# Latent attention with an output layer: VectorE and ScalarE in program order in three of four query blocks, with other tile sets and a later rotary stack

## The chip, the cores and the metric

The kernel runs on one core of a Trainium2 chip. A core has TensorE (PE: matrix products; its weight loads are listed as PEld), VectorE (DVE), ScalarE (ACT), GpSimd (POOL) and SyncE (SP, which here issues most DMAs). Each engine runs its own queue of instructions; semaphores tie them together. The metric is the device time of one execution in microseconds (us). Most executions agree within 0.3%.

## The reference

One transformer layer on x of 2048 rows and 512 columns, all in float32. Cut to what matters:

```python
cq = rms_norm(x @ w_qa.T, q_a_ln_w)                  # latent query, 384
q_nope, q_pe = split((cq @ w_qb.T), 16 heads)        # 128 and 64 per head
ckv = x @ w_kva.T                                    # latent 128 and rotary key 64
k_nope, v = split(rms_norm(ckv[:, :128]) @ w_kvb.T)  # 128 and 128 per head
scores = (q_nope @ k_nope.T + rot(q_pe) @ rot(k_pe).T) * scale, causal
out = softmax(scores) @ v
x = layernorm(x + concat(out) @ w_o.T)
x = layernorm(x + x @ (weight * scale_weight).T + bias)
```

## The kernel before

**What is computed where.** The up-projection of the keys is folded into the query weights, and the one of the values into the output weights (tile `wvo`, made by `value_output` from `wo` and `wv`). So all heads share one latent key and one latent value, and a head's score is a product of its projected query (`qn`) with the latent keys `Kn` plus a product of its rotary query (`pe`) with `Kp`. A float32 factor is split into a high and a low part, and three products replace one. The softmax probabilities become a high and a low float16 half.

**How the work is cut.** The queries fall into four blocks b of 512 rows, the 16 heads into eight pairs p, a block into four query tiles qt of 128 rows. `units` (L609) runs over p, then qt, then the two heads j. One head's 128 queries are called a unit here: a pair has eight units, numbered 2 qt + j. A unit of block b looks at nk = 128 (4b + qt + 1) keys: 128 to 512 in block 0, up to 1024 in block 1, 1536 in block 2, 2048 in block 3.

**A unit, stage by stage.** `head_scores` (L420): PE writes the scores into one or two PSUM tiles of up to 1024 keys (L409, five products for each 512 keys); DVE adds the causal mask where PE has not (L415), takes the row's maximum of each tile (L442) and makes the bias from it (L449 or L451); ACT takes the exponential `pr` of each tile and its sum (L457); DVE makes `inv` from the sums (L467 or L469) and its reciprocal (L470). `head_probs` (L473): ACT writes the high half of `hl` (L478), DVE the low half (L481), both in two cuts when nk is above 1024, and a DMA on SP's queue transposes `hl` into a ring in SBUF (L485). `head_scores` is given the generator of the unit before (`prev`) and draws its steps in among its own. `values` (L534), one to three query tiles later, multiplies the transposed probabilities with V on PE, ACT copies the result `ot` (L539), and a DMA stores it.

**Fillers.** While a pair is worked on, the next pair's queries are projected a piece at a time: `fill` is called after the units whose number is in the list `at`. `project_nope` (L368) has two pieces, one head each (PE L379, then a split by ACT L66 and DVE L67). `project_pe` (L323) has two pieces and serves two pairs at once; after its products on DVE (L340), POOL builds the rotary stack `pe` (L347 to L362) with one copy by ACT (`ph`, L350). At a block's last pair the next block's latent query `cq` and the weights `wq` and `wpe` are loaded on the way (`load_block`, `load_wq`, `load_wpe`). In block 3's last pair the fillers are two pieces of `value_output` (L177), and `prepare_output` (L724) loads `wo` and the first stored results and splits them.

**What sets the order.** Block 0 is ordered by the program's scheduler on all engines. Blocks 1 to 3, and the value projections that start the tail, stand in a `manual_schedule` for PE and SP: these two issue in program order, while the scheduler orders DVE, ACT and POOL by its own estimate. In the tail, PE again runs in a written order: `accumulate` (L743) sums the heads' results times `wvo`, then the normalisation and the second linear layer follow.

**Buffers.** Blocks 1 and 3 have three score tiles of two PSUM banks, block 2 has two of these and two of one bank, and two banks are left for projections and values. All SBUF tiles of a unit in blocks 1 to 3 (`pr`, `hl`) come from the pool `blk13` with two buffers each, beside the ring.

Of the kernel before, what the change touches and what calls it, by code (L numbers as in the profile page):

```python
# [19 lines left out]
P = 128  # L20
# [29 lines left out]
def mla_block(ctx: ExitStack, tc: tile.TileContext, a, out):  # L50
# [272 lines left out]
    def project_pe(b, g, direct=None):  # L323

        if direct is None and ("wpe", b, g) not in state:
            load_wpe(b, g)
        w = state.pop(("wpe", b, g)) if direct is None else direct
        cq, cs = state["cq"], state["cs"]
        prod = prj.tile([P, 2, 2, QB], F32, tag="prod", name=f"prod{b}_{g}")
        for x in range(2):  # L330
            ps = psum["m"].tile([P, QB], F32, tag="m", name=f"ps_pe{b}_{g}_{x}")
            n = 0
            for lt in range(LT):
                for i, k in ((0, 0), (0, 1), (1, 0)):
                    nc.tensor.matmul(  # L335
                        ps, w[:, i, lt, x * P : (x + 1) * P], cq[:, k, lt, :], start=n == 0, stop=n == 8
                    )
                    n += 1
            for k in range(2):
                nc.vector.tensor_tensor(prod[:, k, x, :], ps, cs[:, k ^ x, :], ALU.mult)  # L340
            if x == 0:
                yield
            elif b or g == 3:
                load_wpe(*((b, g + 1) if g < 3 else (b + 1, 0)))
        rp, tp = prod[:, 0], prod[:, 1]
        eng = nc.vector if (b, g) == (0, 0) else nc.gpsimd
        eng.tensor_tensor(rp[:, 0, :], rp[:, 0, :], rp[:, 1, :], ALU.subtract)  # L347
        eng.tensor_tensor(rp[:, 1, :], tp[:, 0, :], tp[:, 1, :], ALU.add)
        ph = prj.tile([P, 2, QB], F32R, tag="ph", name=f"ph{b}_{g}")
        nc.scalar.activation(ph, rp, AF.Copy)  # L350
        pe = blk.tile([P, 4, QB], F32R, tag="pe", name=f"pe{b}_{g}")

        quick = b == 0 or (b, g) == (1, 0)
        for j in range(4):
            q = slice(32 * j, 32 * j + 32)
            for x in range(2):
                to = pe[32 * x : 32 * x + 32, j, :]
                if quick:
                    nc.scalar.activation(to, rp[q, x, :], AF.Copy)
                else:  # L360
                    nc.gpsimd.tensor_copy(to, rp[q, x, :])
                (nc.gpsimd if not quick or (b, g) == (0, 0) and j % 2 else nc.vector).tensor_tensor(  # L362
                    pe[64 + 32 * x : 96 + 32 * x, j, :], rp[q, x, :], ph[q, x, :].bitcast(F32), ALU.subtract
                )
        state["pe", b, g] = pe
        yield

    def project_nope(b, p, direct=None):  # L368
# [5 lines left out]
        for j in range(2):  # L374
            ps = psum["m"].tile([P, QB], F32, tag="m", name=f"ps_qn{b}_{p}_{j}")
            n = 0
            for lt in range(LT):
                for i, k in ((0, 0), (0, 1), (1, 0)):
                    nc.tensor.matmul(  # L379
                        ps, w[:, i, lt, j * P : (j + 1) * P], cq[:, k, lt, :], start=n == 0, stop=n == 8  # L380
                    )
                    n += 1
            split(ps, qn[:, 0, j, :], qn[:, 1, j, :], kvln)
            if j == 1:
                state["qn", b, p] = qn
                if b or p == NPAIR - 1:
                    load_wq(*((b, p + 1) if p + 1 < NPAIR else (b + 1, 0)))
                if p == NPAIR - 1:
                    load_block(b + 1)
            yield  # L390

    def project(b, p):
# [27 lines left out]
    def head_scores(pool, b, p, j, qt, nk, prev):  # L420
# [6 lines left out]
        for ti, ck in enumerate(cks):  # L427

            if b == 2 and ti == 1:
                ps = psum["t"].tile([P, 1, 512], F32, tag="t", name=f"s{b}_{p}_{qt}_{j}_{ti}", bufs=2)  # L430
            else:
                ps = psum["s"].tile(
                    [P, 2, 512], F32, tag="s", name=f"s{b}_{p}_{qt}_{j}_{ti}", bufs=2 if b == 2 else 3
                )
            w = ck[0][1]
            for ci, (c0, w) in enumerate(ck):
# [14 lines left out]
            nc.vector.tensor_scalar(bias, neg[:, 0:1], neg[:, 1:2], r, ALU.min, ALU.mult)  # L451
        for _ in prev:
            pass
        pr = pool.tile([P, nk], F32, tag="pr", name=f"pr{b}_{p}_{qt}_{j}")
        sums = small.tile([P, 2], F32, tag="sums", name="sums")
        for ti, (v, c0, n, w) in enumerate(tiles):
            nc.scalar.activation(  # L457
# [151 lines left out]
    def units(pool, ring, b):  # L609
        lag = min(ring.shape[1] // (2048 * (b + 1)) - 1, 3)  # L610

        for p in range(NPAIR):
# [24 lines left out]
            for qt in range(4):  # L637
# [78 lines left out]

    cuts = {}

    def load_wo(g, tag):
        w = blk.tile([P, 4, HID], F32, tag=tag, name=f"wo{g}")  # L720
        nc.sync.dma_start(w, a["wo"][:, 4 * g : 4 * g + 4])  # L721
        state.setdefault("wo", []).extend(w[:, j] for j in range(4))

    def prepare_output(b, p, k):  # L724
# [39 lines left out]
    blk13 = ctx_m.enter_context(tc.tile_pool(name="blk13", bufs=2, reuse_waits="tile"))  # L764
    ring = blk13.tile([P, 12 * 2048], F16, name="ring", bufs=1)
    side[:] = []
    state["queue"] = nc.sync
    with tc.manual_schedule(engines={mybir.EngineType.PE, mybir.EngineType.SP}):
        for b in range(1, NB):
            with ExitStack() as ctx_s:  # L770
                for k in ("t", "s") if b == 2 else "s":
                    psum[k] = ctx_s.enter_context(
                        tc.tile_pool(name=f"ps_{k}{b}", bufs=1, space=PSUM, reuse_waits="tile")
                    )
                units(blk13, ring, b)

        flush()
        ps_a = ctx.enter_context(tc.tile_pool(name="ps_a", bufs=4, space=PSUM, reuse_waits="tile"))
# [20 lines left out]
    wvo += [pc.tile([P, 2, 2, HID], F32R, name=f"wvo{p}") for p in range(EARLY, NPAIR)]  # L799
    fsc = pc.tile([P, HID], F32, name="fsc")  # L800
    nc.gpsimd.dma_start(fsc, a["fsc"].partition_broadcast(P))
    fb = pc.tile([P, HID], F32, name="fb")
# [53 lines left out]
            if late and next(late[0], None) is None:  # L856
                late.pop(0)

    ET = mybir.EngineType
# [97 lines left out]
```

## Time and profile before

Times of three runs: 1638.54, 1638.7 and 1641.59 us, median 1638.7. The profiled execution is another one:

| what | us |
|---|---|
| profiled execution, its own time | 1642.03 |
| its span in the profile | 1640.2 |
| PE busy | 1562.4 (95%) |
| PEld busy | 1294.7 (79%) |
| DVE busy | 1161.8 (71%) |
| ACT busy | 929.0 (57%) |
| POOL busy | 360.5 (22%) |

The span runs from the first to the last recorded instruction; the execution's time holds 1.8 us more around it. Shares are of the span. Below, a time such as 876.83 is a place in the span. A line such as `PE s L409 <- ACT pr L457: 16.9, 16, 3.6` says that PE, before its instructions of L409 that write `s`, waited for ACT's L457 for 16.9 us in all, in 16 waits, the longest 3.6 us. A timeline line has start, length, engine, line, operation and tiles, and in brackets the idle time before it and what ended that. In the rows by stage, the clock is the one granted to TensorE, 1.00 for full speed.

### The profile page before, as it was taken

Reading aid. Unit: us, or ns where it says so; the run is one execution under the profiler, and the core shown is the slowest. Engines: PE = TensorE matmul, PEld = TensorE weight load, DVE = VectorE, ACT = ScalarE, POOL = GpSimd, SP = SyncE. Lnnn points to the kernel's source line nnn. Section 1 sums busy time; section 2 is a strip of 40 time slices with the busy share of each in tenths; the row PEclk is TensorE's granted clock in tenths of the full one; section 3 lists DMA queues with packets and bytes.
Section 4 is the critical chain, followed back from the end, with each engine's and each line's share of the span. In section 5 each row is a group of like instructions: output and inputs, shape, how many; then the busy total and the mean of one; then the engine's idle time right before and its main releaser. Section 6 shows DMA issues by size and latency. Waiting matters only on the chain. (4 is left out here: it accounts for less than half of the span.)

```text
span 1640.2 us, 24716 instructions
## 1 busy us (share of the span) xinstructions
PE 1562.4 (95%) x9130; PEld 1294.7 (79%) x9130; DVE 1161.8 (71%) x2099; ACT 929.0 (57%) x1631; POOL 360.5 (22%) x434
## 2 busy tenths in 40 slices
PE   8898999999998999999999999999999999999997
PEld 7787877788877888888887787787887777688876
DVE  5677777887778888887787777777777674455554
ACT  5667666666655676766665565565566564311120
POOL 2232324153105405050033202201300000022132
PEclk9899999999999999999999999999999999999999
DMA  6789677788887878888898687786788698433230
GB/s 213 218 218 235 169 186 166 144 168 170 162 189 158 177 160 167 159 165 167 175 187 165 128 162 151 143 157 138 143 155 168 133 183 209 145 114 122 91 109 32
DMA packets 633031, 262.48 MB, mean 160 GB/s; under 512 B 570288, under 2 KB 611376, under 8 KB 631888
## 3 DMA queue, kind: packets, MB, share of 16 engines
q1 hardware_dynamic: 621472, 233.62, 66.4%
q0 software_dynamic: 4672, 17.73, 3.5%
q10 hardware_dynamic: 6768, 9.57, 2.0%
q8 instruction: 72, 1.18, 0.3%
q14 instruction: 47, 0.39, 0.1%
HBM read 83.17 MB, written 35.13 MB: 72 GB/s over the span
## 5 line engine op out<-in xcount | busy, mean ns | idle before, releaser
L409 PE MATMUL s<-Kn,qn 128*128 128x512 f32 (+4 forms) x1920 | 522.9, 378 | 29.6 <-ACT pr L457 27.3
L457 ACT ACTIVATE pr<-s,bias,rq 128x1024 f32<-128x1024 f32 (+3 forms) x320 | 324.3, 1017 | 142.4 <-DVE bias L451 101.5
L409 PEld LDWEIGHTS s<-Kn,qn 128*128 128x128 f32 x1920 | 338.8, 190 | 83.3 <-ACT pr L457 39.6
L534 PE MATMUL o<-ring,V 128*128 128x256 f16 x3252 | 393.6, 273 | 6.9 <-ACT ot L539 3.7
L481 DVE SCALAR_TENSOR_TENSOR hl<-pr,inv,hl 128x1024 f16<-128x1024 f32 (+7 forms) x320 | 357.4, 1137 | 60.3 <-ACT hl L478 58.9
L478 ACT ACTIVATE hl<-pr,inv 128x1024 f16<-128x1024 f32 (+7 forms) x320 | 295.4, 961 | 167.9 <-DMA ring<-hl 60.9
L534 PEld LDWEIGHTS <-V 128*128 128x128 f16 x3264 | 302.7, 98 | 86.6 <-issue 47.3
L442 DVE TENSOR_REDUCE neg<-s 128x1 f32<-128x1024 f32 (+3 forms) x320 | 318.5, 996 | 71.0 <-PE s L409 66.5
L409 PE MATMUL s<-Kp,pe 128*128 128x512 f32 (+4 forms) x1280 | 361.4, 363 | 0.0
L409 PEld LDWEIGHTS s<-Kp,pe 128*128 128x128 f32 x1280 | 234.0, 189 | 29.6
L347 POOL TENSOR_TENSOR prod<-prod 128x512 f32<-128x512 f32 x15 | 19.3, 1284 | 662.2 <-DVE prod L340 662.2
L379 PE MATMUL ps_qn<-cq,wq 128*128 128x512 f32 x576 | 147.0, 401 | 5.1 <-ACT ot L539 4.3
L743 PE MATMUL acc<-wvo,oh 128*128 128x512 f32 x448 | 145.4, 406 | 0.0
L362 POOL TENSOR_TENSOR pe<-prod,ph 32x512 fp32r<-32x512 f32 x92 | 140.7, 1530 | 11.0 <-issue 5.1
L379 PEld LDWEIGHTS ps_qn<-cq,wq 128*128 128x128 f32 x576 | 108.4, 192 | 26.7 <-ACT ot L539 4.8
L743 PEld LDWEIGHTS acc<-wvo,oh 128*128 128x128 f32 x448 | 84.7, 191 | 21.4 <-issue 2.9
L743 PE MATMUL acc<-wvo,ol 128*128 128x512 f32 x224 | 89.2, 398 | 0.0
L469 DVE TENSOR_SCALAR inv<-sums 128x1 f32<-128x1 f32 x128 | 26.9, 210 | 80.1 <-ACT pr L457 80.0
L64 DVE TENSOR_TENSOR ol<-o,oh 128x1024 fp32r<-128x1024 f32 x28 | 38.5, 1376 | 62.6 <-ACT oh L63 62.6
L63 ACT ACTIVATE oh<-o 128x1024 fp32r<-128x1024 f32 x28 | 29.7, 1060 | 93.4 <-PE acc L743 54.1
L335 PE MATMUL ps_pe<-cq,wpe 128*128 128x512 f32 x288 | 71.9, 394 | 3.8 <-DMA cq<-cq_d 3.8
L539 ACT ACTIVATE ot<-o 128x256 f32<-128x256 f32 x128 | 48.1, 377 | 46.0 <-PE o L534 45.9
(140 smaller groups left out, 1608.3 us busy)
## 6 DMA issues: line engine op xcount, KB each, us to landing
wq<-wq_d SPq DMA_DIRECT2D x22, 768.0 KB, 5.6
o<-ot_d SPq DMA_DIRECT2D x32, 512.0 KB, 3.3
ot_d<-ot SPq DMA_DIRECT2D x97, 128.0 KB, 2.5
wpe<-wpe_d SPq DMA_DIRECT2D x10, 768.0 KB, 5.1
wq<-wq_d POOLq DMA_DIRECT2D x9, 768.0 KB, 6.0
wq_d<-wst SPq DMA_DIRECT2D x9, 512.0 KB, 5.0
cq_d<-cqst SPq DMA_DIRECT2D x18, 256.0 KB, 3.8
wo<-in_wo_dram SPq DMA_DIRECT2D x4, 1024.0 KB, 8.2
```

The source lines that it names most:

```text
L64: nc.vector.tensor_tensor(l, ps, h.bitcast(F32), ALU.subtract)
L335: nc.tensor.matmul(ps, w[:, i, lt, x * P : (x + 1) * P], cq[:, k, lt, :], start=n == 0, stop=n == 8)
L362: (nc.gpsimd if not quick or (b, g) == (0, 0) and j % 2 else nc.vector).tensor_tensor(pe[64 + 32 * x : 96 + 32 * x, j, :], rp[q, x, :], ph ...
L379: nc.tensor.matmul(ps, w[:, i, lt, j * P : (j + 1) * P], cq[:, k, lt, :], start=n == 0, stop=n == 8)
L409: nc.tensor.matmul(ps[:, :w], lhs, K[:, i, c0 : c0 + w], start=n == 0, stop=n == 4)
L442: nc.vector.tensor_reduce(neg[:, ti : ti + 1], v, axis=AX.XY, op=ALU.max, negate=True)
L457: nc.scalar.activation(pr[:, c0 : c0 + n * w].rearrange("p (a c) -> p a c", a=n), v, AF.Exp, bias=bias, scale=r, accum_out=sums[:, ti : ti ...
L478: nc.scalar.activation(hl[:, 0, c], pr[:, c], AF.Copy, scale=inv)
L481: nc.vector.scalar_tensor_tensor(hl[:, 1, c], pr[:, c], inv, hl[:, 0, c], ALU.mult, ALU.subtract)
L534: nc.tensor.matmul(ps[:, :256], vt[:, i, k % 4, :], v[:, :, l, k, :], start=n == 0, stop=n == 3 * kts - 1)
L539: nc.scalar.activation(ot, ps[:, :256], AF.Copy)
L743: nc.tensor.matmul(acc, l[:, t, c], state["wvo"][p][:, i, j, :], start=p == 0 and j == 0 and n == 0, stop=p == NPAIR - 1 and j == 1 and n ...
```

## The change

1. In blocks 1 to 3 DVE and ACT, too, issue in program order.
2. `project_pe` gives way once more, after its second product, so the rotary stack is put into the program one filler step later; `load_wpe` stays ahead of it. The lists `at` get a number more or are moved.
3. `load_block` comes ahead of `load_wq`.
4. Each of the blocks 1 to 3 has a pool of its own. `pr` has 4 buffers in block 1 and 2 in the others, `hl` has 6, 4 and 2 in blocks 1, 2 and 3. The ring has its own pool. A block ends with the rest of its last unit (`flush`).
5. In block 3 the three score tiles are taken in turn from a tile set of two and one of one, so that the first uses other banks than before.
6. The second `wo` load comes at unit 4 of block 3's last pair into a place of its own, the two splits of stored results come a unit earlier, the third one's split after the last values, and the places of three other tiles move.

```diff
             for k in range(2):
                 nc.vector.tensor_tensor(prod[:, k, x, :], ps, cs[:, k ^ x, :], ALU.mult)
-            if x == 0:
+            if x and (b or g == 3):
+                load_wpe(*((b, g + 1) if g < 3 else (b + 1, 0)))
+            if x == 0 or b and (b, g) != (1, 0):
                 yield
-            elif b or g == 3:
-                load_wpe(*((b, g + 1) if g < 3 else (b + 1, 0)))
...
             if j == 1:
                 state["qn", b, p] = qn
+                if p == NPAIR - 1:
+                    load_block(b + 1)
                 if b or p == NPAIR - 1:
                     load_wq(*((b, p + 1) if p + 1 < NPAIR else (b + 1, 0)))
-                if p == NPAIR - 1:
-                    load_block(b + 1)
...
-                ps = psum["s"].tile(
-                    [P, 2, 512], F32, tag="s", name=f"s{b}_{p}_{qt}_{j}_{ti}", bufs=2 if b == 2 else 3
+                k = "s"
+                if b == 3:
+                    state["turn"] = (state.get("turn", -1) + 1) % 3
+                    k = "ssu"[state["turn"]]
+                ps = psum[k].tile(
+                    [P, 2, 512], F32, tag=k, name=f"s{b}_{p}_{qt}_{j}_{ti}", bufs=3 if b == 1 else 1 if k == "u" else 2
                 )
...
-        pr = pool.tile([P, nk], F32, tag="pr", name=f"pr{b}_{p}_{qt}_{j}")
+        pr = pool.tile([P, nk], F32, tag="pr", name=f"pr{b}_{p}_{qt}_{j}", bufs=4 if b == 1 else 2)
...
-        hl = pool.tile([P, 2, nk], F16, tag="hl", name=f"hl{b}_{p}_{qt}_{j}")
+        hl = pool.tile([P, 2, nk], F16, tag="hl", name=f"hl{b}_{p}_{qt}_{j}", bufs=(6, 4, 2)[b - 1])
...
             if p + 1 == NPAIR:
-                at = (1, 2, 4, 5) if b < NB - 1 else (1, 3, 5, 7)
-            elif p % 2 == 0 and p + 2 < NPAIR:
-                at = (0, 1, 2, 3) if (b, p) == (1, 0) else (0, 1, 3, 4)
+                at = (1, 2, 3, 4, 6) if b < NB - 1 else (1, 3, 5, 7)
+            elif p + 2 == NPAIR:
+                at = (1, 3)
+            elif p % 2 == 0:
+                at = (0, 1, 2, 3, 4) if (b, p) == (1, 0) else (0, 2, 3, 4, 6)
             else:
-                at = (3, 4)
+                at = (3, 5)
...
             drain()
+        if b:
+            flush()
...
             if k == 1:
-                load_wo(0, "qn")
+                load_wo(0, blk, "qn")
             if k in (2, 3):
                 latent_load(0, k - 2)
-            if k in (6, 7):
-                cuts[0, k - 6] = latent_split(0, k - 6)
+            if k == 4:
+                load_wo(1, state["pcr"], "wo")
+            if k in (5, 6):
+                cuts[0, k - 5] = latent_split(0, k - 5)
...
-    with tc.manual_schedule(engines={mybir.EngineType.PE, mybir.EngineType.SP}):
+    ET = mybir.EngineType
+    with tc.manual_schedule(engines={ET.PE, ET.SP, ET.DVE, ET.Activation}):
         for b in range(1, NB):
             with ExitStack() as ctx_s:
-                for k in ("t", "s") if b == 2 else "s":
+                for k in ("s", "ts", "us")[b - 1]:
...
-                units(blk13, ring, b)
+                blkb = ctx_s.enter_context(tc.tile_pool(name=f"blk{b}", bufs=2, reuse_waits="tile"))
+                units(blkb, ring, b)
...
             if p == 0:
-                load_wo(1, "pe")
-                cuts[0, EARLY] = latent(0, EARLY)
-                load_wo(2, "qn")
-                load_wo(3, "qn")
+                latent_load(0, EARLY)
+                load_wo(2, blk, "pe")
+                load_wo(3, blk, "qn")
...
         while vals:
             half_values()
+        cuts[0, EARLY] = latent_split(0, EARLY)
         put_in(True)
```

More of the change, by code (lines that the diff above doesn't have):

```diff
@@ L717, in mla_block, with load_wo @@
     cuts = {}
-    def load_wo(g, tag):
-        w = blk.tile([P, 4, HID], F32, tag=tag, name=f"wo{g}")
+    def load_wo(g, pool, tag):
+        w = pool.tile([P, 4, HID], F32, tag=tag, name=f"wo{g}", bufs=1 if tag == "wo" else 2)
         nc.sync.dma_start(w, a["wo"][:, 4 * g : 4 * g + 4])
@@ L763, in mla_block @@
     psum["m"] = ctx_m.enter_context(tc.tile_pool(name="ps_m", bufs=2, space=PSUM, side="right", reuse_waits="tile"))
-    blk13 = ctx_m.enter_context(tc.tile_pool(name="blk13", bufs=2, reuse_waits="tile"))
-    ring = blk13.tile([P, 12 * 2048], F16, name="ring", bufs=1)
+    ring = ctx_m.enter_context(tc.tile_pool(name="rings", bufs=1, reuse_waits="tile")).tile(
+        [P, 12 * 2048], F16, name="ring"
+    )
     side[:] = []
     state["queue"] = nc.sync
-    with tc.manual_schedule(engines={mybir.EngineType.PE, mybir.EngineType.SP}):
+    ET = mybir.EngineType
+    with tc.manual_schedule(engines={ET.PE, ET.SP, ET.DVE, ET.Activation}):
         for b in range(1, NB):
             with ExitStack() as ctx_s:
-                for k in ("t", "s") if b == 2 else "s":
+                for k in ("s", "ts", "us")[b - 1]:
                     psum[k] = ctx_s.enter_context(
@@ L798, in mla_block @@
     pc = ctx.enter_context(tc.tile_pool(name="pc", bufs=1, reuse_waits="tile"))
-    wvo += [pc.tile([P, 2, 2, HID], F32R, name=f"wvo{p}") for p in range(EARLY, NPAIR)]
+    wvo += [pc.tile([P, 2, 2, HID], F32R, name=f"wvo{p}") for p in range(EARLY, NPAIR - 1)]
+    wvo.append(state["pcr"].tile([P, 2, 2, HID], F32R, tag="wo", name="wvo7", bufs=1))
     fsc = pc.tile([P, HID], F32, name="fsc")
@@ L857, in advance @@
                 late.pop(0)
-    ET = mybir.EngineType
     CUT = 2
```

## The prediction

> **What bounds the kernel now.** I read the table of busy time by stage first (one row per stretch: PE, PEld, DVE, ACT and POOL busy, granted clock, DMA share, GB/s). The stretches are block 0, block 1, block 2, block 3 and the last value projections:
>
> ```profile
> 0.00:263.90 263.90, 233.50 (x1513) 199.09 (x1514) 185.85 (x429) 175.08 (x446) 81.67 (x152) 0.97 0.76 205
> 263.90:516.10 252.20, 238.84 (x1433) 201.42 (x1431) 198.83 (x415) 151.39 (x241) 83.40 (x74) 0.99 0.81 165
> 516.10:876.80 360.70, 355.80 (x2148) 299.46 (x2148) 291.19 (x547) 244.06 (x439) 83.61 (x72) 1.00 0.84 168
> 876.80:1372.00 495.20, 481.86 (x2925) 395.65 (x2925) 354.39 (x514) 304.39 (x441) 61.48 (x54) 1.00 0.77 151
> 1372.00:1420.00 48.00, 43.03 (x195) 31.04 (x194) 18.20 (x24) 14.44 (x20) 1.11 (x2) 0.93 0.78 228
> ```
>
> PE is busy nearly all the time, and its work stays the same (9130 matmuls). So what can be won is PE's idle time, some 70 us in all, and what can be lost is new idle time. Counted from PE's instructions in the trace, the gaps are 30.4 us in block 0 (which the change hardly touches), 13.4 in block 1, 1.3 in block 2, 16.9 in block 3 with its entry, 5.0 in the last value projections and 3.3 at the end. The view of waits says who ends them; columns are total, times, longest. Block 1:
>
> ```profile
> ACT hl L478 <- DMA ring<-hl: 43.0, 30, 6.1
> PE s L409 <- ACT pr L457: 9.8, 6, 4.4
> ```
>
> Block 3:
>
> ```profile
> ACT pr L457 <- DVE bias L451: 80.2, 51, 5.6
> DVE inv L469 <- ACT pr L457: 64.6, 53, 2.4
> PE s L409 <- ACT pr L457: 16.9, 16, 3.6
> ```
>
> PE waits for score banks, banks wait for the exponentials, and those wait for the bias on DVE, or in block 1 for the hl buffer held by a transpose. The timeline of one unit of block 3 (start, length) shows how the bias comes late:
>
> ```profile
> 930.60 1.23 DVE L442 TENSOR_REDUCE neg<-s 128x1 f32<-128x1024 f32 x1 [1.04 <-PE s L409]
> 931.74 2.34 DVE L481 SCALAR_TENSOR_TENSOR hl<-pr,inv,hl 128x960 f16<-128x960 f32 x2
> ...
> 934.00 0.27 DVE L451 TENSOR_SCALAR bias<-neg,rq 128x1 f32<-128x1 f32 x1
> 934.36 1.21 ACT L457 ACTIVATE pr<-s,bias,rq 128x1024 f32<-128x1024 f32 x1 [2.63 <-DVE bias L451]
> ...
> 935.71 0.96 PE L409 MATMUL s<-Kn,qn 128*128 128x512 f32 x3 [0.50 <-ACT pr L457]
> ```
>
> The scheduler ran both low halves of the head before ahead of this unit's bias; ACT stood for 2.63 us, and PE for 0.50.
>
> **Part 1: DVE and ACT in program order.** No instruction is added. DVE's order per unit u becomes: reduce 0, one low half of u-1, mask, reduce 1, bias, the other low half of u-1, inv, reciprocal, then the filler's products. DVE now stands at inv until ACT's exponentials are done. Behind it stand the next unit's reduces, and PE's banks and ACT's exponentials wait for those. So each unit is a chain DVE, ACT, DVE, whose length I add up from start-to-start times in the trace. Block 2, 1536 keys: reduce 1.14, low half .93, mask .20, second reduce .64, bias to exponential .35, exponentials 1.20 and .66, accumulator read and wake .22, inv .25, reciprocal to the next reduce .16: 5.75 us. The same sum gives 4.83, 5.14 and 5.44 for 1152, 1280 and 1408 keys, so 42.3 us for a pair's eight units. The filler adds two qn products (.88 each) and on average two rotary ones (.60 each): 45.3, or 45.9 if each costs a further wake. Eight pairs are 362 to 367 us. PE's own work is 355.8, so **in block 2 the chain becomes the bound**: against 360.7 now that is +2 to +6. I take +4, with ends -2 (fillers hidden in waits) and +12 (a tenth of a microsecond more per unit).
>
> Block 1 by the same sum: units of 2.69, 2.94, 3.18 and 3.42, so 24.5 a pair and 27.3 with fillers: 218 against PE's 238.8. Block 3: 5.85, 6.17, 6.47 and 6.78, so 54.3 a pair with fillers and masks: 434 against PE's 481.9. There PE stays the bound, and the chain's slack (.33 us a unit in block 1, .75 in block 3) covers the new wait.
>
> In block 3 the bias comes one low half earlier, .65 to .85 us. That covers the .50 of each pair, and most of the .91 that follows it (7 pairs, 9.9 us in all). A gap of 3.48 at 1340.90, where ACT and DVE stood on splits that waited for loads, shrinks to about 1.2, because splits no longer stand ahead of an exponential that is ready. I keep 3 of the 13.3 us inside block 3: **-10.3** (ends -13 and -5).
>
> **Part 2: tile sets.** In block 1 hl has 6 buffers instead of 2 and pr 4. The 43.0 us of ACT waits for transposes go, since a transpose is 1.5 to 3.5 us on SP's queue and the buffer is now used again six units later. PE's short waits in block 1 (pairs of .74 and .97, .47 and 1.24) go with them. The gap of 4.36 at 516.07 was ACT behind such a hl and a late bias; now PE waits only for two exponentials, about 1.0 us. The cq load, put ahead of the wq load, takes most of the 2.34 before 483.29. So 13.4 becomes about 2.4: **-11** (ends -13 and -4). In block 2 hl has 4 buffers; its 17.9 us of such waits on ACT touch no PE gap now, so I count nothing; they return in block 2's chain only if two buffers were too few.
>
> **Part 3: bank order.** Block 3 starts on the bank of block 2's next-to-last unit; the 3.59 us before 876.83 become at most 1. Block 2's window of 360.7 holds that gap, and my +4 runs to block 3's first score, so this is inside the +4.
>
> **Part 4: rotary stack a head later, cq load first.** PE's work only moves by a unit. At the end of block 0 the gaps of 1.51 (cq load) and 3.74 (at 263.05, ACT busy with casts) shrink to some .3 and 2: **-3** (ends -5 and +1). The stack of block 2's first rotary group comes a unit, 3.75 us, later on POOL. It ended for the first head near 504.1, for the last at 513.56, and is needed at about 512.9 for the first: 508 fits.
>
> **The clock.** Two stretches that follow a gap, of 4.36 and of 3.59 us:
>
> ```profile
> 516.70:520.10 3.40, 3.40 (x12) 3.40 (x12) 1.61 (x4) 2.08 (x3) 0.00 (x0) 0.50 1.15 260
> 876.90:880.30 3.40, 3.40 (x18) 2.85 (x19) 2.31 (x5) 1.91 (x3) 0.00 (x0) 1.00 0.87 44
> ```
>
> The clock falls to half for 3.41 us after some gaps, a loss of 1.7. It did so after 3.74, 4.36, 2.85 and 2.12, not after 3.59 or 3.48. Without the 4.36 one dip goes, **-1.7**; the one at 264 goes perhaps, **-1**. (The Trainium skill, "TensorE: Matmul & The Clock Gate", section "Why this matters for your kernels", asks for no idle gaps above some 3 us. By it the gaps of 2.85 and 2.12 would have cost nothing and those of 3.59 and 3.48 a dip each; the trace disagrees four times, and by the rule my sum would lose 1.7 us more of old dips.)
>
> **Part 5: the last value projections.** The load of wo1 (1 MB) comes 35 us earlier, which frees 2.5 to 4.2 us of queue. But ACT's order now puts the split of o0_2 and o0_3 ahead of wvo2's copy. o0_3 landed at 1399.67, perhaps 1396 now; wvo2's copy began at 1392.83 and would begin near 1397. PE then stands about 4 us longer at ps_wo, while the second stop (2.12, at 1402.73) goes with its dip: **+3** (ends -3 and +6).
>
> **The sum.** -3 - 1 - 11 - 1.7 + 4 - 10.3 + 3 = -20 us, against the profiled execution of 1642.03 (span 1640.2): 1622. The median of the runs shown is 3.3 below the profiled one, so **1618.5**.
>
> **Rivals.**
> A, all covers hold: block 2 at PE's pace (-2 instead of +4), tail -3, half of what I left in blocks 1 and 3 gone too: -36, or 1603. For it: before, block 2 ran at 357 with the same chain between units. Against: DVE there is busy 291 of 361 and gains a wait of some 2 us a unit.
>
> B, slower: the chain through DVE's inv is longer than my sum, by x a unit. One mechanism: everything on DVE waits behind inv or behind a filler product whose projection PE has not finished (ACT's wait for PE's projection is up to 2.3 us in block 2, 14.8 in all). Block 2 pays 64x, block 1 from x = .33 and block 3 from .75. At x = .36 the gain of 20 and the 3.3 below are spent: 23 + 2. At x = .5 it is 32 + 11, so 1641.5. (The Trainium skill, "PSUM — Partial Sum Buffer", section "Engine vs sequencer instructions", states that the queues of ScalarE and VectorE are strict FIFO, which speaks against this change: a waiting inv holds all that is behind it. No row here shows a reduce passing a waiting inv. By the rule block 2 pays the chain, +4; could reduces pass, it would run at PE's pace, and the sum would be some 6 us lower.)
>
> C, it does little: the scheduler's order was near program order, so that only buffers count: -11 to -5 in blocks 0 and 1, block 2 +4, nothing in block 3: about -6, or 1632.5.
>
> D, transfers: earlier loads and four or six hl tiles in flight crowd the DMA engines (share .81 to .84 now), so transposes land late and values wait: a 10% longer transpose, 3.49 to 3.84, is covered by a lag of one to three query tiles. Free; if not, near the old time.
>
> **How the numbers follow.** Forecast (1610 to 1627) .47, A .17, C .15, D and "no effect" .07, B .14. Range 1601 to 1637: it takes in A, C and half of D. About 0.2%, 3.3 us, is what can be told from no change. Faster .78, same .08, slower .14.
>
> **What would show it.** Block 1's gaps under 4 us, and no wait of ACT for a transpose. In block 2, DVE's wait for inv grows from 15.4 to over 100 us, and PE shows many waits of s for pr, 6 to 11 us in sum. In block 3 PE's wait for pr falls under 6. No half clock near 516. In the tail, a PE stop over 4 us before ps_wo. Block 2 over 372 us long, or PE waits for pr in block 1, would prove me wrong.

## The result and the profile after

The changed kernel takes 1639.47 us (median of 12 runs, 1637.79 to 1644.69), the kernel before 1638.47 (median of 12 runs, 1631.97 to 1641.6). The ratio is 1.0013, with a 95% interval of 1.0 to 1.0026: no change, where 1618.5 was forecast. The profiled execution has a span of 1638.1 us against 1640.2.

That the time stayed does not mean that nothing happened. Here are the stages of the changed kernel, in the same columns as the rows of before (block 0, 1, 2, 3, last value projections):

```profile
0.00:260.89 260.89, 235.27 (x1514) 199.88 (x1515) 183.50 (x424) 172.50 (x441) 82.46 (x152) 0.96 0.77 205
260.89:504.28 243.39, 237.11 (x1432) 200.24 (x1430) 207.86 (x421) 156.69 (x247) 83.64 (x72) 1.00 0.85 173
504.28:889.53 385.25, 360.89 (x2151) 301.20 (x2149) 294.51 (x540) 240.84 (x432) 87.78 (x75) 0.99 0.75 154
889.53:1369.50 479.97, 475.64 (x2901) 395.54 (x2898) 363.00 (x517) 301.65 (x442) 64.74 (x54) 1.00 0.81 160
1369.50:1418.00 48.50, 40.70 (x202) 29.82 (x203) 20.10 (x26) 16.13 (x24) 1.11 (x2) 0.93 0.72 208
```

The second column is the length of the stage. Block 1 went from 252.2 to 243.4 and block 3 from 495.2 to 480.0, with PE busy for nearly all of both. Block 2 went from 360.7 to 385.3, and PE stands still for 24.4 us of it, where it stood for 4.9 before. By these rows the gains of blocks 1 and 3, 24.0 us, were given back in block 2, almost to the microsecond.

For the rest of this text a stage runs from a block's first score product to the next block's, block 3 to its own last one; so cut, the stages can be compared between kernels:

| kernel | block 0 | 1 | 2 | 3 | rest | span | median us |
|---|---|---|---|---|---|---|---|
| before | 263.9 | 252.1 | 360.8 | 489.4 | 274.0 | 1640.2 | 1638.47 |
| changed | 260.9 | 243.4 | 385.3 | 477.4 | 271.2 | 1638.1 | 1639.47 |
| e1 block 2 scheduled | 257.3 | 243.4 | 359.7 | 474.9 | 272.3 | 1607.6 | 1610.0 |
| e2 low halves after the bias | 260.3 | 243.4 | 354.6 | 472.7 | 270.0 | 1600.9 | 1602.16 |
| e3 before, with the order alone | 258.6 | 264.6 | 405.1 | 474.4 | 273.2 | 1675.9 | 1678.1 |
| e4 changed, without the order | 258.2 | 243.7 | 360.9 | 489.5 | 270.5 | 1622.8 | 1621.93 |
| e5 quarter stack | 261.0 | 243.5 | 381.9 | 475.0 | 273.3 | 1634.7 | 1637.41 |
| e6 mask on PE | 259.8 | 243.6 | 365.9 | 473.9 | 274.4 | 1617.5 | 1618.14 |
| e7 two hl buffers | 260.0 | 259.9 | 390.2 | 475.3 | 273.9 | 1659.3 | 1660.11 |
| e8 e2 with another tail | 260.4 | 243.6 | 354.6 | 472.7 | 269.2 | 1600.4 | 1601.69 |
| e9 stack at once | 257.5 | 248.2 | 390.4 | 479.9 | 268.6 | 1644.6 | 1647.22 |
| e10 e2 with the old loads | 261.0 | 240.8 | 354.2 | 472.7 | 270.6 | 1599.3 | 1600.02 |
| e11 e2, also in block 3 | 259.0 | 243.5 | 354.6 | 471.0 | 269.0 | 1597.2 | 1600.03 |
| e12 DVE's order only | 259.2 | 240.1 | 383.9 | 480.8 | 268.7 | 1632.8 | 1634.58 |
| e13 no POOL stack | 260.6 | 243.5 | 378.2 | 477.4 | 272.6 | 1632.2 | 1633.68 |

Block 0 and the rest differ by some us between kernels whose code is the same there: before and e3 by 5.3 us in block 0, the changed kernel and e9 or e5 by 2 to 3 in the rest. Smaller differences in these two columns say nothing.

The waits of the changed kernel in block 2:

```profile
ACT pr L462 <- DVE bias L456: 118.0, 60, 3.5
DVE inv L474 <- ACT pr L462: 76.3, 63, 1.9
...
PE o L539 <- ACT ot L544: 15.8, 11, 2.9
...
PE s L409 <- ACT pr L462: 6.8, 10, 1.0
...
DVE neg L447 <- PE s L409: 0.6, 1, 0.6
```

And the same waits in the kernel before, from the views of ACT and of DVE:

```profile
ACT pr L457 <- DVE bias L451: 21.3, 17, 2.5
...
DVE neg L442 <- PE s L409: 17.8, 23, 1.3
DVE inv L469 <- ACT pr L457: 15.4, 13, 2.0
```

ACT waits for the bias once in nearly every unit, and DVE for the exponentials once in nearly every unit: 21.3 and 15.4 us have become 118.0 and 76.3. That is a chain of two engines that take turns. DVE no longer waits for PE's scores (.6 us, 17.8 before), so PE has next to no part in the chain. PE's own waits, for ACT's copy `ot` and for `pr`, follow from it.

Block 3 shows the same picture on DVE, but there PE has enough to do:

```profile
ACT pr L462 <- DVE bias L456: 156.2, 63, 4.6
DVE inv L474 <- ACT pr L462: 82.5, 64, 2.3
...
PE s L409 <- ACT pr L462: 4.1, 3, 2.9
```

PE's 16.9 us of waits for `pr` have become 4.1. The waits of ACT and DVE are longer than before and cost little (e11 below puts it at 1.7 us).

### The profile page after: what moved, and what is told of

The parts are those of the page before. It is cut to its first block, busy times and chain, and to the rows that moved or that the text cites. A ratio compares the mean times of both kernels' runs of the same rounds, so it can differ in the third digit from the quotient of the medians.

```text
span 1638.1 us, 24741 instructions
## 1 busy us (share of the span) xinstructions
PE 1560.8 (95%) x9130; PEld 1297.0 (79%) x9130; DVE 1182.9 (72%) x2099; ACT 928.6 (57%) x1631; POOL 369.3 (23%) x434
## 5 line engine op out<-in xcount | busy, mean ns | idle before, releaser
L409 PE MATMUL s<-Kn,qn 128*128 128x512 f32 (+4 forms) x1920 | 521.9, 377 | 16.5 <-ACT pr L462 12.4
L486 DVE SCALAR_TENSOR_TENSOR hl<-pr,inv,hl 128x1024 f16<-128x1024 f32 (+7 forms) x320 | 363.8, 1137 | 10.8 <-ACT hl L483 8.7
L447 DVE TENSOR_REDUCE neg<-s 128x1 f32<-128x1024 f32 (+3 forms) x320 | 317.6, 993 | 26.5 <-PE s L409 19.8
L362 POOL TENSOR_TENSOR pe<-prod,ph 32x512 fp32r<-32x512 f32 x92 | 145.4, 1581 | 11.0 <-issue 5.1
L361 POOL CAST pe<-prod 32x512 fp32r<-32x512 f32 x88 | 68.6, 779 | 3.3
L335 PEld LDWEIGHTS ps_pe<-cq,wpe 128*128 128x128 f32 x288 | 54.9, 195 | 17.6 <-DMA cq<-cq_d 4.2
```

The source lines that it names most:

```text
L335: nc.tensor.matmul(ps, w[:, i, lt, x * P : (x + 1) * P], cq[:, k, lt, :], start=n == 0, stop=n == 8)
L409: nc.tensor.matmul(ps[:, :w], lhs, K[:, i, c0 : c0 + w], start=n == 0, stop=n == 4)
L447: nc.vector.tensor_reduce(neg[:, ti : ti + 1], v, axis=AX.XY, op=ALU.max, negate=True)
L486: nc.vector.scalar_tensor_tensor(hl[:, 1, c], pr[:, c], inv, hl[:, 0, c], ALU.mult, ALU.subtract)
```

## The experiments

The diffs of e8, e10 and e11 are against e2; all others against the changed kernel, but for e3, which is against the kernel before. "..." stands for lines left out.

Two theories were set against each other. Theory 1: block 2 runs at the length of the chain that program order makes. Theory 2: the fillers' places, the later stack or the tile sets made block 2 longer.

**e1: block 2's DVE and ACT ordered by the scheduler, all else as changed.**

```diff
-    with tc.manual_schedule(engines={ET.PE, ET.SP, ET.DVE, ET.Activation}):
-        for b in range(1, NB):
+    for b in range(1, NB):
+        with tc.manual_schedule(engines={ET.PE, ET.SP} if b == 2 else {ET.PE, ET.SP, ET.DVE, ET.Activation}):
...
+    with tc.manual_schedule(engines={ET.PE, ET.SP, ET.DVE, ET.Activation}):
         flush()
```

> The changed kernel, but in block 2 alone DVE and ACT are ordered by the scheduler again; tile sets, fillers and loads stay as changed. Theory 1 (block 2 runs at the length of its chain DVE, ACT, DVE in program order): block 2 falls from 385 us to 357 to 364, DVE's wait of inv for pr there falls from 76 us to below 30, the whole kernel takes about 1616. Theory 2 (the fillers' places, the later rotary stack or the tile sets made block 2 longer, not the order): block 2 stays above 378 and the kernel at 1633 or more.

Measured: block 2 takes 359.7 us, DVE waits 15.7 us for the exponentials, the kernel takes 1610.0 (ratio 0.9816, 0.9787 to 0.9845). The time is some 6 us under what theory 1 gave, the stage is as it gave. Theory 1 holds, theory 2 falls: with the changed fillers, stacks and tile sets, the order alone decides in block 2.

What the scheduler does in block 2 is seen in the timeline of the kernel before, DVE alone:

```profile
642.25 0.27 DVE L451 TENSOR_SCALAR bias<-neg,rq 128x1 f32<-128x1 f32 x1
643.70 1.22 DVE L442 TENSOR_REDUCE neg<-s 128x1 f32<-128x1024 f32 x1 [1.18 <-PE s L409]
644.84 0.20 DVE L469 TENSOR_SCALAR inv<-sums 128x1 f32<-128x1 f32 x1
644.97 0.29 DVE L415 TENSOR_TENSOR s<-s,maskb 128x128 f32<-128x128 f32 x1
645.16 0.15 DVE L470 RECIPROCAL inv<-inv 128x1 f32<-128x1 f32 x1
```

Between a unit's bias and its inv it puts the next unit's first reduce, while ACT makes the exponentials. A count over block 2 finds the next unit's reduce ahead of the reciprocal in 45 of 64 units before, in 49 in e1, and in none in the changed kernel.

**e2: program order, but both low halves of the unit before behind this unit's bias.**

```diff
             if ti < nt - 1:
                 next(prev, None)
-                next(prev, None)
+                if b != 2:
+                    next(prev, None)
```

> The changed kernel, but in block 2 both low halves of the unit before stand behind this unit's bias on DVE, where DVE stands idle for 1.2 us a unit waiting for the exponentials. Theory 1: the chain loses one low half, .73 to .93 us a unit, 52 us over 64 units; PE's own 356 to 361 becomes the bound again: block 2 takes 359 to 368 and the kernel 1615 to 1622. Theory 2: block 2 stays above 378. A third reading, that the low halves only move the wait (they end after the exponentials and inv comes as much later): block 2 370 to 385.

Measured: block 2 takes 354.6, less than expected, and the kernel 1602.16 (ratio 0.9764, 0.9735 to 0.9794). The timeline of DVE in one unit of e2 shows the pause filled:

```profile
605.70 0.27 DVE L457 TENSOR_SCALAR bias<-neg,rq 128x1 f32<-128x1 f32 x1
605.89 1.53 DVE L487 SCALAR_TENSOR_TENSOR hl<-pr,inv,hl 128x576 f16<-128x576 f32 x2
607.94 0.21 DVE L475 TENSOR_SCALAR inv<-sums 128x1 f32<-128x1 f32 x1 [0.52 <-ACT pr L463]
```

DVE stands for .52 us ahead of inv where the changed kernel stands for 1.24 (below). Over block 2 that wait is 19.7 us, in place of 76.3. Program order was not wrong as such; one instruction stood on the wrong side of the bias. And PE's own work is 353.6 us of the stage:

```profile
503.60:858.20 354.60, 353.57 (x2150) 298.40 (x2148) 302.96 (x545) 242.95 (x433) 87.35 (x75) 1.00 0.85 169
```

**e3: the kernel before with only the order changed; e4: the changed kernel without it.**

```diff
-    with tc.manual_schedule(engines={mybir.EngineType.PE, mybir.EngineType.SP}):
+    with tc.manual_schedule(engines={mybir.EngineType.PE, mybir.EngineType.SP, mybir.EngineType.DVE, mybir.EngineType.Activation}):
```

> The kernel before with nothing changed but DVE and ACT in program order in blocks 1 to 3. Theory 1: block 2 goes from 361 to 375 to 390; block 1, with two hl buffers, gets no gain (ACT stands at hl for the transpose, now with all behind it): 250 to 275; block 3 falls from 495 by 5 to 15. Together 1640 to 1665. Theory 2: block 2 stays at 361 and the kernel is at or below 1635.

> The changed kernel with DVE and ACT ordered by the scheduler again in blocks 1 to 3; everything else stays as changed. Theory 1: block 2 at 357 to 364; block 1 keeps most of its gain through the six hl buffers (243 to 249); block 3 goes back to 488 to 496. Together 1618 to 1630. Theory 2: block 2 above 378, so 1635 to 1650.

Measured: e3 1678.1 (ratio 1.0237, 1.0194 to 1.0279), longer than expected: block 2 reaches 405.1. e4 takes 1621.93 (0.9889, 0.9859 to 0.9919), as expected in every stage. Together they divide the change: the order alone is worth -15 us in block 3, +12 in block 1 and +44 in block 2; without it, the rest of the change keeps the whole gain of block 1 (243.7) and loses nothing in block 2.

**e5, e13: how much of block 2's chain is POOL's doing.** e5 writes the stack for one head of four, which all heads of block 2 then use; e13 leaves out all of POOL's work for the three stacks made within block 2 that block 2 uses, and its scores take the first one. Both give another result in block 2.

```diff
-        for j in range(4):
+        for j in range(1 if b == 2 else 4):
...
-        qp = pe[:, 2 * (p % 2) + j, qs]
+        qp = pe[:, 0 if b == 2 else 2 * (p % 2) + j, qs]
```

> The changed kernel with three quarters of the rotary stack of block 2 left out: POOL copies and subtracts for one head of four, and all heads of block 2 use that one, so the result of block 2 differs; the products, the copy by ACT and the order of DVE and ACT are unchanged. Theory: a low half on DVE that runs beside POOL takes longer (1.27 us against .91 on average, 10.4 us in block 2), and in program order that stands on the chain. Then block 2 falls from 385 to 376 to 380 and the low halves of 640 keys that took 1.84 take .85. Rival: the long low halves have another cause (ACT's reads of the same tile, transposes), or the wait for inv takes up what is won: block 2 at 384 to 386.

Measured: block 2 at 381.9, 3.4 less. The 640-key low half still took longest beside POOL's sums, which e5 keeps. Block 2 lay between theory and rival, so e13 followed:

```diff
+        if b == 2 and g:
+            ph = prj.tile([P, 2, QB], F32R, tag="ph", name=f"ph{b}_{g}")
+            nc.scalar.activation(ph, rp, AF.Copy)
+            state["pe", b, g] = state["pe", 2, 0]
+            yield
+            return
         eng.tensor_tensor(rp[:, 0, :], rp[:, 0, :], rp[:, 1, :], ALU.subtract)
```

> The changed kernel without any of POOL's work for the three rotary stacks made within block 2 (the two sums and all copies and subtracts are left out, and the scores use the stack of the block's first group, so block 2's result differs); DVE, ACT and PE keep every instruction and their order. Theory: the low halves beside POOL are the part of the chain that my sum left out, about 2.7 us for each even pair (unit 3's gap to the next reciprocal 7.43 against 5.28 and 1.35 for two products, units 4 and 6 .3 and 1.0 more): pairs 0, 2 and 4 fall from 50.8 to 47.8 to 48.4 and block 2 from 385.3 to 376 to 378. Rival: with a quarter of the stack left the gain was 3.4; if the sums cost nothing, the whole is about 4.5 and block 2 stays at 380 to 382.

Measured: block 2 at 378.2, 7.1 less; pairs 0, 2 and 4 went from 50.8 us to 48.5, just outside what was expected. So POOL costs 2.4 us in each pair with a stack. The timeline of the changed kernel (no PE, no SP) shows how:

```profile
624.39 1.30 POOL L348 TENSOR_TENSOR prod<-prod 128x512 f32<-128x512 f32 x1
624.53 1.84 DVE L486 SCALAR_TENSOR_TENSOR hl<-pr,inv,hl 128x640 f16<-128x640 f32 x1
625.63 3.00 POOL L361 CAST pe<-prod 32x512 fp32r<-32x512 f32 x3
...
627.26 0.90 DVE L486 SCALAR_TENSOR_TENSOR hl<-pr,inv,hl 128x640 f16<-128x640 f32 x1
```

A narrower window of it shows the cast that runs at 627.26:

```profile
626.88 0.60 POOL L361 CAST pe<-prod 32x512 fp32r<-32x512 f32 x1
```

And DVE in the same unit of e13:

```profile
621.89 0.88 DVE L492 SCALAR_TENSOR_TENSOR hl<-pr,inv,hl 128x640 f16<-128x640 f32 x1
```

A low half that starts .14 us after POOL's sum takes 1.84 instead of .88. The sum has 1.16 us left then; the low half is .96 longer. The second low half starts when a cast has .22 left and takes .90, .02 longer. So a low half is longer by what is left of the POOL instruction that runs when it starts, less about .2, and the kind of instruction does not matter. Counted over all 15 traces, 938 of 944 low halves that start while POOL adds, casts or subtracts 512 columns fit this within .05 us; the other six start at the very end of one such instruction, with the next one less than .06 us away. It works the other way, too: the cast that starts at 627.52, while the second low half runs, takes 1.10 instead of .61. (The Trainium skill, "SBUF — State Buffer", section "SBUF: two separate sides", states that a DVE instruction with two SBUF inputs and a GpSimd instruction that reads SBUF lock each other out for a whole instruction. The 1.84 beside a sum, the .90 beside a cast near its end and the 1.10 of the cast behind it agree with that.)

**e6: block 2's mask by PE instead of DVE.**

```diff
-        by_product = b == 0 or b == 3 and j == 0
+        by_product = b in (0, 2) or b == 3 and j == 0
```

> The changed kernel with block 2's causal mask added by one small product on PE instead of by DVE. My sum gave DVE's mask .20 us in the chain; the changed kernel's timeline shows .32 from its start to the reduce behind it. By .32 over 64 units block 2 falls by 20 us to 363 to 368, by .20 to 371 to 374. Rival: the mask is hidden (DVE waits later for inv anyway): 383 to 387. PE gains 64 products of about .1 to .2 us, 6 to 13 us, which count only where PE is the bound.

Measured: block 2 at 365.9, 19.4 less, or .30 a unit; the kernel takes 1618.14 (0.9878, 0.985 to 0.9906). Most units without fillers and without POOL beside them are .33 shorter, at every number of keys (from one reciprocal to the next 5.21 against 4.88 at 1280 keys, 5.91 against 5.58 at 1536). The mask's price in the chain was .3, not .2.

**e7: two hl buffers everywhere.**

```diff
-        hl = pool.tile([P, 2, nk], F16, tag="hl", name=f"hl{b}_{p}_{qt}_{j}", bufs=(6, 4, 2)[b - 1])
+        hl = pool.tile([P, 2, nk], F16, tag="hl", name=f"hl{b}_{p}_{qt}_{j}", bufs=2)
```

> The changed kernel with two hl buffers in every block, as before, instead of 6, 4 and 2. Theory: with program order the buffers are what keep ACT, and behind it the whole chain, from waiting for transposes: block 1 goes from 243 to 258 to 268, block 2 from 385 to 398 to 408, block 3 stays at 475 to 480: 1665 to 1685. Rival: the fillers' places and the later rotary stack gave block 1 its gain: block 1 stays below 250 and the kernel below 1650.

Measured: block 1 at 259.9, so six buffers are worth 16.5 us there under program order; the rival is out. Block 2 only at 390.2, not 398 or more: four buffers are worth 5 us. e3's further 15 us in block 2 come from what e7 keeps of the change; e9 below gives 5 of them to the stack's place, the rest was not divided.

**e8: e2 with another order in the tail.** The copies of wvo2 and wvo3 stand ahead of the split of o0_3.

```diff
+    with tc.manual_schedule(engines={ET.PE, ET.DVE, ET.Activation}):
+        latent_load(0, EARLY + 1)
+        for p in (EARLY, EARLY + 1):
+            for _ in value_output(p, ps_f, "ff"):
+                pass
+        cuts[0, EARLY + 1] = latent_split(0, EARLY + 1)
...
-            else:
-                for p in (EARLY, EARLY + 1):
-                    for _ in value_output(p, ps_f, "ff"):
-                        pass
...
-                cuts[nxt] = latent(*nxt)
+                if nxt not in cuts:
+                    cuts[nxt] = latent(*nxt)
```

> The kernel with block 2's low halves behind the bias, and in the tail the copies of wvo2 and wvo3 put ahead of the split of o0_3 on ACT and DVE. Theory: the stop of 3.62 us at ps_wo (and .73 after it) is ACT behind the split that waits for its load, and the half clock follows it: the stretch from block 3's last score to the end falls from 270.0 by 3 to 6 and the kernel goes to 1596 to 1600. Rival: wo or the later load is what PE waits for, or the later split of o0_3 stops PE a little after: no gain, within 1.5 us.

Measured: 1601.69 us; the rest takes 269.2 against 270.0, within what it varies by itself. The number is the rival's: the stop of 3.62 us that e2 has there is gone, but PE now stands at other places, in the timeline of e8:

```profile
1363.41 0.69 DVE L826 TENSOR_TENSOR fraw<-fraw,fsc 128x512 f32<-128x512 f32 x1 [3.23 <-DMA fsc<-in_fsc_dram]
...
1366.33 1.12 PE L177 MATMUL ps_wo<-wo,wv 128*128 128x512 f32 x2 [2.19 <-DVE wvo L67]
```

DVE stands 3.23 us for the load of `fsc`, with a copy of wvo behind it that PE needs; PE stands 2.19 us for that copy.

**e9: the stack at once, in the filler step of its second product.**

```diff
-            if x == 0 or b and (b, g) != (1, 0):
+            if x == 0:
                 yield
```

and the step for the stack taken out of the lists `at`.

> The changed kernel with the rotary stack right behind its second product again, in the same filler step (the products and the other projections stay at their units). Theory: in program order ACT's copy ph then stands behind POOL's two sums of 1.28 and 1.30 us, and the next unit's work on ACT behind ph, so each of the stacks in block 2 lengthens the chain by up to 2.6 us: block 2 from 385 to 391 to 396, blocks 1 and 3 by at most 4 each (slack). Rival: the stack's place costs nothing, as my sum had it: block 2 within 1.5 of 385.3.

Measured: block 2 at 390.4 (+5.1), block 1 at 248.2 (+4.8), the kernel at 1647.22 (1.0052, 1.003 to 1.0073). The mechanism is the expected one; its price is a little under what was expected in block 2 and a little over it in block 1. In the timeline of e9, ACT and DVE:

```profile
629.38 1.06 ACT L350 ACTIVATE ph<-prod 128x1024 fp32r<-128x1024 f32 x1 [3.86 <-POOL prod L348]
630.34 1.53 ACT L483 ACTIVATE hl<-pr,inv 128x640 f16<-128x640 f32 x2
631.19 0.88 DVE L486 SCALAR_TENSOR_TENSOR hl<-pr,inv,hl 128x640 f16<-128x640 f32 x1 [2.90 <-ACT hl L483]
```

ACT stands 3.86 us at `ph` for POOL's sums, the high half behind it comes late, and DVE stands 2.90 us for that.

**e10: e2 with wq loaded ahead of the next block's cq, as before.**

```diff
-                if p == NPAIR - 1:
-                    load_block(b + 1)
                 if b or p == NPAIR - 1:
                     load_wq(*((b, p + 1) if p + 1 < NPAIR else (b + 1, 0)))
+                if p == NPAIR - 1:
+                    load_block(b + 1)
```

> The kernel with block 2's low halves behind the bias, with wq loaded ahead of the next block's cq again. My prediction gave cq first 1.2 us before block 1 and most of 2.3 before block 2. Theory: stops of PE before ps_pe of 1.5 to 2.5 us come back at both places and a shorter one before block 3: 3 to 6 us more, 1605 to 1608. Rival: cq's landing isn't what PE waits for, or only block 0's end changes: within 1.5 us.

Measured: 1600.02 us. The theory falls; the order of these loads is worth nothing here. With cq first, PE stands 4.0 us for cq at 238.4 of e2; without, it stands 3.8 us for an ot at 259.3 of e10.

**e11: both low halves after the bias in block 3, too.**

```diff
-                if b != 2:
+                if b == 1:
                     next(prev, None)
```

> As the kernel with block 2's low halves behind the bias, and the same in block 3. Theory (block 3 is bound by PE, its chain has slack): block 3 stays at 472.7 within 1.5 us, though each unit's chain loses .8 to 1.2 us. Rival (the chain still sets part of block 3): block 3 falls by 3 to 10.

Measured: block 3 at 471.0 against 472.7, just past the bound that was given, and 1600.03 us against 1602.16 in all. Taking a low half out of each unit's chain, .8 to 1.2 us by the expectation, brings 1.7 us in 64 units: PE is the bound there.

**e12: program order for DVE, but not for ACT.**

```diff
-    with tc.manual_schedule(engines={ET.PE, ET.SP, ET.DVE, ET.Activation}):
+    with tc.manual_schedule(engines={ET.PE, ET.SP, ET.DVE}):
```

> The changed kernel with only DVE, PE and SP in program order in blocks 1 to 3, ACT ordered by the scheduler. Theory: it is DVE standing at inv that makes the chain; block 2 stays at 382 to 388. Rival: ACT's order makes a good part of it (the copies ot and ph ahead of hl): block 2 at 365 to 378.

Measured: block 2 at 383.9. e4, which differs from it in DVE's order alone, takes 360.9. It is DVE's order that makes the chain.

The fastest kernels here are e2, e8, e10 and e11, at 1600 to 1602 us; their ratios to before are 0.9747 to 0.9774, and their intervals overlap.

## Why the prediction was wrong

**The step that failed is the sum of the chain in block 2.** It named the right bound ("in block 2 the chain becomes the bound") and gave it +4 us with an upper end of +12; measured are +24.5. The recorded sign of being wrong, block 2 over 372 us, came. All other stages together gave -26.5, against the -24 forecast. That these agree is partly luck: block 1 gave 2.3 less than forecast, block 3 1.7 more, and the stretch behind block 3 came out at -2.8 instead of +3, within what it varies by itself.

The chain was short by two terms.

First, times from a start to the next start were taken where an unrelated instruction followed. The mask's .20 is such a time: before, a low half stands behind it. In the changed order its own reduce does. One unit of the changed kernel, DVE:

```profile
616.93 0.17 DVE L475 RECIPROCAL inv<-inv 128x1 f32<-128x1 f32 x1
617.01 1.21 DVE L447 TENSOR_REDUCE neg<-s 128x1 f32<-128x1024 f32 x1
618.13 0.81 DVE L486 SCALAR_TENSOR_TENSOR hl<-pr,inv,hl 128x576 f16<-128x576 f32 x1
618.86 0.29 DVE L415 TENSOR_TENSOR s<-s,maskb 128x128 f32<-128x128 f32 x1
619.18 0.42 DVE L447 TENSOR_REDUCE neg<-s 128x1 f32<-128x256 f32 x1
619.64 0.27 DVE L456 TENSOR_SCALAR bias<-neg,rq 128x1 f32<-128x1 f32 x1
619.84 0.81 DVE L486 SCALAR_TENSOR_TENSOR hl<-pr,inv,hl 128x576 f16<-128x576 f32 x1
621.89 0.21 DVE L474 TENSOR_SCALAR inv<-sums 128x1 f32<-128x1 f32 x1 [1.24 <-ACT pr L462]
622.13 0.17 DVE L475 RECIPROCAL inv<-inv 128x1 f32<-128x1 f32 x1
```

From the mask to the reduce that reads what it wrote it is .32, and from that reduce of 256 keys to its bias .46, where rows of before gave .34 between starts. With one place that is shorter (the reciprocal to the next reduce .08, not .16), a unit is .16 longer by these three. e6, which takes the mask away and gains .33 in such units, confirms the first of them; the second was only read.

Measured from one reciprocal to the next, units without fillers and without POOL beside them take 5.46 and 5.10 us at 1152 keys (first and second head), 5.21 and 5.28 at 1280, 5.58 at 1408 (second head), 5.82 and 5.91 at 1536. The prediction had 4.83, 5.14, 5.44 and 5.75. With 5.58 for both heads at 1408 that is 1.6 us a pair more, 13 us in eight pairs. Units of 1280 keys and more are .07 to .16 over their sum, about what the three terms give. Those of 1152 keys are .63 and .27 over their sum: the first has .20 more because DVE waits there for ACT's high half, and low halves of 768 keys from the unit before; what is left of it stays open.

Second, POOL. The low halves were priced at rows beside which POOL did not work. e13 shows 2.4 us for each pair with a stack, 7.1 for three pairs. The fourth stack made in block 2, that of block 3, was not taken away, but the three units that are longer beside a stack have the same lengths there (7.44, 6.42 and 6.79 us in e13 itself), so it is 9.4 in all. That excess is in the profile of before as well (a mean of 1148 ns for 640 keys, longer than the 972 for 704), off the chain there.

Together 13 and 9.4 are 22 us. The sum stood at 362 us before the choice of +4, so it was 23 short. The fillers' products were priced right: a qn product adds .86 to .93 us to nearly every unit that has one, two rotary products 1.1 to 1.2.

Rival B was set at the right price. The chain is longer than what was taken by x = (385.3 - 364.8) / 64 = .32 a unit, where B put the point of no gain at .36. (Its figure for x = .5 does not follow from its own terms: 32 + 11 on 1618.5 is 1661.5.) That all on DVE waits behind inv is what happened; the mechanism that B named, a filler whose projection PE has not finished, was not it: DVE waited 2.5 us in all of block 2 for ACT's qn copies. B deserved more than .14, since the chance that a sum of ten start-to-start times is 6% short was the largest risk in the text.

**Point by point.**
- Block 1, -11: measured -8.7, and by the mechanism named. PE still stands 6.3 us there, where 2.4 were forecast and under 4 was the recorded sign. ACT's wait for transposes is gone, e7 shows what the buffers are worth, e4 that the order is not needed. The 2.34 us before 483 went, but not through the load order (e10).
- Block 3, -10.3: measured -12.0, by the order (e3, e4).
- Banks: from block 2's last score to block 3's first 5.2 us before, 1.4 in the changed kernel; 5.5 in e3, which has the old banks. Right.
- Stack a head later, counted as nothing: wrong under program order. e9 shows that it is worth 5 us in block 2 and 5 in block 1, because ACT otherwise stands at `ph`. Without it the forecast would have been missed by more.
- cq first, -3: the profile shows -3.0 for block 0, but e3, with that edit left out, shows -5.3, and e10 shows no loss without it; the stop only moved. The forecast of .3 us for cq's wait was 3.7 short.
- Clock: no half clock at 264 or near 505, as forecast. But the one near 516 lay in block 2, whose length the chain sets, so that its -1.7 had nothing to shorten. And new ones came after other stops. Two lie in block 2, from 534.29 and from 810.77, each 3.41 us long, after stops of PE of 2.93 and 2.26 us; one of 6.83 us, from 237.33, comes with the stop for cq. Two more:

```profile
1397.20:1404.80 7.60, 4.48 (x7) 2.04 (x8) 3.99 (x6) 2.08 (x4) 0.00 (x0) 0.55 0.75 278
896.10:899.50 3.40, 3.40 (x12) 2.88 (x11) 2.35 (x4) 1.76 (x2) 0.00 (x0) 0.50 1.14 212
```

  The second follows a gap of 2.89 us. What decides it is worked out in the last section.
- Tail, +3: the stop before ps_wo came from the cause named (ACT and DVE behind the split of o0_3), but it is 3.63 us, .8 more than before and not about 4 more. The second did not go; it is 3.07, with DVE behind a load of the second linear layer's weight. The stretch itself took .5 us more, the whole rest 2.8 less, within what it varies by. e8 shows that the stop moves when its cause is taken away.

## What to carry to other kernels

Program order on an engine that must wait for its partner once per step makes a chain; add up that chain with the durations that its instructions have behind and beside their new neighbours (a result read at once, an instruction of POOL that runs when they start), and compare it with the bound in each stage, since a stage with 1% of slack pays all that a stage with 10% hides. When the chain is too long, look for work that stands ahead of the hand-over and may stand behind it: here one low half moved across the bias turned no change into 2.4%. An edit that looks free in a scheduled kernel (a stack a step later, more buffers) can be what makes program order bearable, so such edits are priced together.

## What the runs showed of the hardware

**A result read at once.** A DVE instruction that reads what the one ahead of it on DVE has just written starts about .1 us later than an unrelated one: .32 against .20 behind a mask of 128 by 128, .46 against .34 behind a reduce of 256 keys, .59 against .47 behind one of 384, all in the kernel before.

**DVE beside POOL.** A low half of 640 keys in block 2 of the changed kernel took .88 us alone. It took .87 to .90 in the eight cases where the POOL instruction that ran at its start had .10 to .22 us left, 1.82 to 1.85 in the four where 1.13 to 1.16 were left, and 1.30 in the four where a cast of .61 began within .02 us of it. At 704 keys the low halves took .94 to .95, and 1.92 to 1.93 in the four where a subtract had just begun. In all these it is what is left of POOL's instruction, less about .2.

**The half clock.** The length of a stop alone does not decide: half clock came after stops of 2.12 and 2.85 us in the kernel before and of 2.26, 2.89 and 2.93 in the changed one, and not after 3.48 and 3.59 in the kernel before. The places do. Half clock starts at 264.11, 516.70, 1393.92 and 1404.16 in the kernel before, and these are 74, 257 and 3 steps of 3.4133 us apart. So time is cut into cells of that length, and what counts is how much of one cell PE stands. The stop of 2.12 has 1.98 us in the cell before 1404.16 (58% of it), the one of 2.85 has 2.41 in the cell before 1393.92 (71%). The stop of 3.48 is cut at 1339.31 into 1.89 and 1.59 us (55% and 47%), the one of 3.59 at 875.10 into 1.86 and 1.73 (54% and 51%). In each of the 15 traces the half clock keeps to such a grid, with a start of its own. From 40 us on, of the cells at full clock, all 98 in which PE stood for 56% or more were followed by half clock, and none in which it stood for under 47%; between these both occurred. Where the grid lies differs from run to run, so whether a stop of 2 to 3.6 us costs a half clock is partly chance.
